# A gated cross-attention and ternary feed-forward block: fewer small instructions, w3 in fp16, one more batch element in Strassen's form

## The chip, the cores and the metric

The kernel runs on one core of a Trainium2 chip. The metric is the device time of one execution in microseconds (us), taken as the median of three runs; the profile is of one more execution. The engines are named as in the profile: PE (TensorE matmuls), PEld (its weight loads), DVE (VectorE), ACT (ScalarE), POOL (GpSimd) and SP (SyncE, whose queue issues every DMA here).

## The reference

The input x is 8 batch elements of 256 x 512, and so is the context. All is float32. Cut to what matters:

```python
# attention, per element; n = layernorm(x), m = context
theta = theta_w @ m + b;  phi = phi_w @ n + b;  g = g_w @ n + b     # latent 128 x 512 each
p     = softmax(theta.T @ phi)                                      # 512 x 512
t     = (p @ g.T).T                                                 # 128 x 512
h     = relu((t - mean(t)) * rsqrt(var(t) + 1e-5) * gamma + beta)
x     = x + tanh(g_xattn) * (out_w @ h + out_b + m)
# feed-forward with ternary weights and 8-bit activations, per row; y = layernorm(x)
bit(y, w) = quant8(rmsnorm(y)) @ ternary(w).T    # ternary: round(w / mean|w|) clipped to -1..1, times mean|w|
x     = x + tanh(g_ffn) * bit(silu(bit(y, w1)) * bit(y, w2), w3)    # w1, w2: 2048 x 512; w3: 512 x 2048
```

## The kernel before

Each batch element b (0 to 7) is held as two tiles of 128 rows by 512 (`x`, `med`). The feed-forward works on 128 rows at a time, numbered i = 2b + c from 0 to 15. All weights are loaded once, scaled, rounded to -1, 0 or 1 and kept on the chip.

The code records about 1500 labelled steps, such as `jtheta0:2` (a projection for element 2), `ug1:7` (the gate matmuls of i = 7, columns 512 to 1023) or `us1:7` (their Silu). A list written out in the source, `order`, says in which sequence the steps are issued, over all engines; each engine runs its own steps in that sequence. A table `alt` puts a step on another engine than its first choice (`v` DVE, `p` POOL, `a` ACT). Tiles come from pools with a fixed number of places by size: `t` (2 KB a partition, 31 places), `f` (4 KB, 7) and `b` (8 KB, 7). A step that takes a place waits until the last reader of what lay there is done, and the instructions behind it on its engine wait with it. That holds for loads in SP's queue too.

The steps that the text speaks of, with their lines in the profile:

- Loads: `x`, `med` (`Lx`, `Lm`), w2T, w1T, w3T in four chunks of 1 MB each (L283, L284).
- Weights: a chunk's sum of absolute values (`ws`, L296 on ACT, L297 on DVE), scaling to int16 (`wr`, L313, L314), sign (`wq`, L320 on ACT, L321 on DVE). w1's and w2's forms are fp16, w3's fp8. For fp8, sums and scaled values go into scratch tiles of 4 KB from pool `f` (`wj`, `wr`); for fp16 they are written where the result goes.
- Attention: layernorm (`nr` L347, `nm` L349, `nx` L352), splits into a high and a low part (`xh`, `xl`, `mh`, `ml`), projections L385, scores L463, maximum L472, exponential L475. For elements 0 and 1 the probabilities are transposed by PE (`pT`, L498), for the others by a DMA (`pt`, L525). Then the mean and variance over the element (L572 to L578, `tr` on L577), output projection L610 with residual L621.
- Feed-forward in: `im` (L651) makes the negated mean, L659 and L661 the statistics, `iz` (L667) the quantized rows, `if` (L680) two scale factors per half, the first of which the Silu reads, `ig` (L682) the reciprocal of the second. A DMA transposes the rows (`it`, L684).
- Up: gate and up matmuls with 512 columns (`fgp`, `fup`, L699), Silu (L709, ACT), product (L711, DVE).
- Quantization of the hidden rows: sum of squares L731, maximum L732, `qf` (L733) and `qe` (L737) from the reciprocal, L734, L735, `qr` L738, power L739, `qb` L740, then scaling `qz` (L745) and a DMA transpose (`qt`, L763).
- Down: 16 matmuls with 512 columns (`fop`, L772, steps `dm`) and a residual (L777). For elements 2 to 6 ("fast") the two halves of an element and the halves of w3 are taken as a 2 x 2 block product in Strassen's form (Winograd's variant): seven products `tP1` to `tP7` of 8 matmuls with 256 columns (`dp`, L857), four sums of the rows (`tS`, L845 on DVE, L846 on POOL), a copy `tC` (L870), four adds from PSUM (`tU`, L864) and two scaled adds (`tA`, L890 on DVE, L892 and L893 on POOL). The sums of w3's blocks (`w3t`; `tW`, L822 on POOL, L823 on DVE) are made once and take one `b` tile for the whole run.

PSUM has eight places of 512 columns, shared by all of PE's results.

```python
_upd(CFG, {..., "bufs": {"t": 31, "f": 7, "b": 7}, "fast": [2, 3, 4, 5, 6], "alt": {...}, "order": [...]})
def tiny(label, fn):
    op(label, v=lambda: fn(V), p=lambda: fn(G))     # a small step, on DVE unless alt says POOL
```

Of the kernel before, what the change touches and what calls it, by code (L numbers as in the profile page):

```python
# [19 lines left out]
P = 128  # L20
# [69 lines left out]
def flamingo_gated_block(  # L90
# [74 lines left out]


    xs = [[w_(f"x{b}_{c}", [P, T]) for c in range(DC)] for b in range(B)]
    meds = [[w_(f"med{b}_{c}", [P, T]) for c in range(DC)] for b in range(B)]
    proj_w = {n: c_(f"{n}_w", [P, DC, L]) for n in ("theta", "phi", "g")}
    proj_src = {"theta": theta_wT, "phi": phi_wT, "g": g_wT}  # L170

    cols, tg = c_("cols", [P, columns.shape[1]]), c_("tg", [P, 2])
    col = {n: (lambda k=k: cols()[:, k : k + 1]) for k, n in enumerate(("theta", "phi", "g"))}
    ob = lambda: cols()[:, 3 : 3 + DC]
    gates = lambda: cols()[:, 3 + DC : 5 + DC]
    gam, bet, ow = c_("gam", [P, T]), c_("bet", [P, T]), c_("ow", [P, D])
    ones, neg_half = c_("ones", [P, P]), c_("neg_half", [P, 2 * DC])

    fac = {n: (c_(f"{n}_max", [P, DC]), c_(f"{n}_sum", [P, 1]), c_(f"{n}_back", [P, 1]), c_(f"{n}_fwd", [P, 1])) for n in ("phi", "g")}
    half_w = {n: c_(f"{n}_half", [P, 2, DC, L], F16) for n in ("phi", "g")}  # L180
    theta_hi, theta_lo = c_("theta_whi", [P, DC, L], F32R), c_("theta_wlo", [P, DC, L], F32R)
    cols2 = c_("cols2", [P, 2])
    bias = {"theta": (lambda: cols2()[:, 0:1]), "phi": (lambda: cols2()[:, 1:2])}

    whole_x = [b for b in range(B) if b not in CFG["xsplit"]]
    whole_m = [b for b in range(B) if b not in CFG["msplit"]]
    assert set(whole_x) <= set(whole_m)
    keep = {"phi": False, "g": any(b not in CFG["p32"] for b in whole_x), "theta": any(b not in whole_x for b in whole_m)}
    scaled_t = {n: c_(f"{n}_sc", [P, DC, L]) if k else w_(f"{n}_sc", [P, 2 * DC, L]) for n, k in keep.items()}
# [19 lines left out]
    def constants():  # L209
        op("C:ones", lambda: V.memset(ones(), 1.0))  # L210
        op("C:half", lambda: V.memset(neg_half(), -0.5))
        if CFG["p32"] or CFG["rpe"]:
            op("C:id0", lambda: G.memset(ident(), 0.0))
            op(
                "C:id1",
                lambda: G.affine_select(
                    out=ident(), in_=ident(), compare_op=ALU.not_equal, fill=1.0, base=0, pattern=[[-1, P]], channel_multiplier=1
                ),
            )
        wps = ps_("warm")  # L220

        op("C:warm", lambda: [PE.matmul(wps()[:, 0:P], ones(), ones(), start=True, stop=True) for _ in range(CFG["warm"])])
        for n in ("theta", "phi", "g"):
            load_proj(n)
        op("Lc:0", lambda: nc.sync.dma_start(out=cols(), in_=columns))
        op("Lgam:0", lambda: nc.sync.dma_start(out=gam(), in_=ln_gamma))
        op("Lbet:0", lambda: nc.sync.dma_start(out=bet(), in_=ln_beta))
        op("Low:0", lambda: nc.sync.dma_start(out=ow(), in_=out_wT))
        op("C:tanh", lambda: S.activation(tg(), gates(), AF.Tanh))
        if CFG["rpe"]:  # L230
            tiny("C:gid", lambda e: e.tensor_scalar(gident(), ident(), tg()[:, 0:1], 1.0, ALU.mult, ALU.mult))

        tiny("C:ow", lambda e: e.tensor_scalar(ow(), ow(), tg()[:, 0:1], 1.0, ALU.mult, ALU.mult))
        op("C:owh", a=lambda: S.copy(ow_hi(), ow()), v=lambda: V.tensor_copy(ow_hi(), ow()))
        tiny("C:owl", lambda e: e.tensor_tensor(ow_lo(), ow(), ow_hi().bitcast(F32), ALU.subtract))
        tiny("C:ob", lambda e: e.tensor_scalar(ob(), ob(), tg()[:, 0:1], 1.0, ALU.mult, ALU.mult))

        for n in ("phi", "g"):
            mx, sm, back, fwd = fac[n]
            tot = ps_(f"{n}_tot")
            op(f"C:{n}max", lambda n=n, mx=mx: V.tensor_reduce(mx(), proj_w[n](), AX.X, ALU.max, apply_absolute_value=True))
            op(f"C:{n}sum", lambda mx=mx, sm=sm: V.tensor_reduce(sm(), mx(), AX.X, ALU.add))
            op(f"C:{n}tot", lambda sm=sm, tot=tot: PE.matmul(tot()[:, 0:1], ones(), sm(), start=True, stop=True))
            lim = 1e-30 if n == "phi" else 1e-2
            op(f"C:{n}back", lambda tot=tot, back=back, lim=lim: V.tensor_scalar(back(), tot()[:, 0:1], lim, 1.0 / G_SCALE, ALU.max, ALU.mult))
            op(f"C:{n}fwd", lambda back=back, fwd=fwd: V.reciprocal(fwd(), back()))
            tiny(f"C:{n}w", lambda e, n=n, fwd=fwd: e.tensor_scalar(scaled_w[n](), proj_w[n](), fwd(), 1.0, ALU.mult, ALU.mult))  # L250
            op(
                f"C:{n}h",
                a=lambda n=n: S.copy(half_w[n]()[:, 0], scaled_w[n]()),
                v=lambda n=n: V.tensor_copy(half_w[n]()[:, 0], scaled_w[n]()),
            )
            tiny(f"C:{n}l", lambda e, n=n: e.tensor_tensor(half_w[n]()[:, 1], scaled_w[n](), half_w[n]()[:, 0], ALU.subtract))
        pback, pfwd = fac["phi"][2:]
        tiny("C:tw", lambda e: e.tensor_scalar(scaled_w["theta"](), proj_w["theta"](), pback(), 1.0, ALU.mult, ALU.mult))
        tiny("C:tb", lambda e: e.tensor_scalar(cols2()[:, 0:1], col["theta"](), pback(), 1.0, ALU.mult, ALU.mult))
        tiny("C:pb", lambda e: e.tensor_scalar(cols2()[:, 1:2], col["phi"](), pfwd(), 1.0, ALU.mult, ALU.mult))  # L260
        op(
            "C:th",
            a=lambda: S.copy(theta_hi(), scaled_w["theta"]()),
            v=lambda: V.tensor_copy(theta_hi(), scaled_w["theta"]()),
        )
        tiny("C:tl", lambda e: e.tensor_tensor(theta_lo(), scaled_w["theta"](), theta_hi().bitcast(F32), ALU.subtract))
        tiny("C:gback2", lambda e: e.tensor_scalar(gback(), fac["g"][2](), 1.0 / P_SCALE, 1.0, ALU.mult, ALU.mult))
# [4 lines left out]
    def weights(n):  # L272
# [30 lines left out]
        if n < 2:  # L303
            op(f"wf:{n}", lambda: V.tensor_scalar(wfac()[:, n : n + 1], wmean()[:, n : n + 1], 1.0 / (127.0 * Q_UNIT), None, ALU.mult))
        else:
            op(f"wf:{n}", lambda: V.tensor_scalar(wmean()[:, 2:3], wmean()[:, 2:3], tg()[:, 1:2], None, ALU.mult))
# [22 lines left out]
    def attention(b):  # L329
        xt, med = xs[b], meds[b]  # L330
        xsp, msp, osp = b in CFG["xsplit"], b in CFG["msplit"], b in CFG["osplit"]
        s32, p32 = b in CFG["s32"], b in CFG["p32"]

        w32 = {
            "phi": proj_w["phi"],
            "theta": scaled_w["theta"] if xsp else proj_w["theta"],
            "g": proj_w["g"] if p32 else scaled_w["g"],
        }
        bias_b = bias if xsp else col

        mv, rstd, nmu = s_("mv", f"mv{b}", [P, DC, 2]), s_("rstd", f"rstd{b}", DC), s_("nmu", f"nmu{b}", DC)
        xn = [w_(f"xn{b}_{c}", [P, T]) for c in range(DC)]
        for c in range(DC):
            st = s_("bst", f"bst{b}_{c}", V.BN_STATS_DIM)
            op(f"nb{c}:{b}", lambda c=c, st=st: V.bn_stats(st(), xt[c]()))  # L345
            op(f"na{c}:{b}", lambda c=c, st=st: V.bn_aggr(mv()[:, c, :], st()))
        tiny(f"nr:{b}", lambda e: e.tensor_scalar(rstd(), mv()[:, :, 1], LN_EPS, 1.0, ALU.add, ALU.mult))  # L347
        op(f"np:{b}", lambda: G.tensor_tensor(rstd(), rstd(), neg_half()[:, :DC], ALU.pow))
        tiny(f"nm:{b}", lambda e: e.tensor_scalar(nmu(), mv()[:, :, 0], -1.0, 1.0, ALU.mult, ALU.mult))  # L349

        def norm(eng, c):
            return eng.tensor_scalar(xn[c](), xt[c](), nmu()[:, c : c + 1], rstd()[:, c : c + 1], ALU.add, ALU.mult)  # L352

# [240 lines left out]
        else:  # L594
# [4 lines left out]
                p=lambda: G.tensor_scalar(h(), h(), 3e38, 0.0, ALU.min, ALU.max),  # L599
            )  # L600

        osums = sums[b] = []
        for c in range(DC):
            o = ps_(f"o_ps{b}_{c}")

# [28 lines left out]
    def ffn_in(b):  # L634
# [10 lines left out]

        for c in range(DC):
            sq = w_(f"fsq{b}_{c}", [P, T])  # L650
            tiny(f"im{c}:{b}", lambda e, c=c: e.tensor_scalar(nmu()[:, c : c + 1], sums[b][c](), -1.0 / T, 1.0, ALU.mult, ALU.mult))  # L651
# [308 lines left out]
```

## Time and profile before

| | before |
|---|---|
| median of three runs (lowest to highest) | 280.13 us (279.75 to 280.41) |
| the profiled execution | 279.37 us |
| its span, first to last instruction | 277.6 us |
| granted clock of PE | 0.999 |
| PE, DVE, ACT, POOL busy | 271.3, 254.0, 227.6, 205.9 us |
| HBM read, written | 22.02 MB, 4.19 MB |

The profile lists what each engine did and when. "Busy" is the union of an engine's instructions; the time that PE's matmuls end is modelled, so its busy share is an upper bound. A group's line gives source line, engine, operation, the tiles and shapes, how often (x), then the busy time in us, the mean duration of one in ns, and the engine's idle time before them. The list of waits gives the engine and line that waited, what ended the wait, the total in us, the number and the longest. The chain of waits is followed back from the last instruction; in order of time each piece has its start and length in us.

### The profile page before, as it was taken

How to read it: one execution, taken by the hardware profiler on the slowest of the kernel's cores; microseconds unless marked ns; L12 is line 12 of the kernel's file. 1: busy time of each engine (PE TensorE's matmuls, PEld its weight loads, DVE VectorE, ACT ScalarE, POOL GpSimd, SP SyncE). 2: the span in 40 equal slices, each digit the busy share in tenths (PEclk: the TensorE clock that was granted, in tenths of full speed). 3: DMA queues.
4: the chain of work that ended last, by engine and by line, in shares of the span. 5: the costliest groups of instructions: out<-in, count | busy, mean ns of one | idle time of the engine just before them, and what ended most of it. 6: DMA issues, size and time to landing. Idle time of an engine off the chain costs nothing.

```text
span 277.6 us, 4741 instructions
## 1 busy us (share of the span) xinstructions
PE 271.3 (98%) x1574; PEld 166.9 (60%) x1574; DVE 254.0 (91%) x537; ACT 227.6 (82%) x337; POOL 205.9 (74%) x273
## 2 busy tenths in 40 slices
PE   7999999999899999999999999999999999999995
PEld 7458585564365555545754778655545566457863
DVE  3798988999999989989999899997999889999895
ACT  1399999999989999899999899895867789675910
POOL 2588774799999998867896989758785855873461
PEclk9999999999999999999999999999999999999999
DMA  7999979998761325134948815916372356605685
GB/s 217 357 347 374 387 277 367 184 195 327 154 115 38 79 41 110 40 76 130 155 97 180 161 41 113 154 34 118 88 142 76 61 130 113 151 2 110 77 211 212
DMA packets 81528, 43.30 MB, mean 156 GB/s; under 512 B 67936, under 2 KB 69088, under 8 KB 81504
## 3 DMA queue, kind: packets, MB, share of 16 engines
q1 hardware_dynamic: 81504, 43.00, 62.2%
q8 instruction: 12, 0.20, 0.3%
q14 instruction: 12, 0.10, 0.1%
HBM read 22.02 MB, written 4.19 MB: 94 GB/s over the span
## 4 chain that ended last, share of the span: by engine, by line
PE 82%; DVE 8%; ACT 3%; issue 2%; DMA 2%; POOL 1%; SPq 0%; POOLq 0%; ACTq 0%
PE fup L699 18%; PE fgp L699 17%; PE dp L857 10%; PE fop L772 6%; PE av L538 4%; PE sc L463 4%; PE phi_ps L385 4%; PE theta_ps L385 3%; PE gx_ps L416 3%; PE tp L498 3%; PE o_ps L610 3%; PE sc L461 3%; PE av L551 3%; DVE nmax L472 2%; DMA med<-in_media 2%
## 5 line engine op out<-in xcount | busy, mean ns | idle before, releaser
L699 PEld LDWEIGHTS <-fqt 128*128 128x128 f16 x512 | 49.0, 99 | 56.8 <-issue 3.2
L699 PE MATMUL fgp<-w1q,fqt 128*128 128x512 f16 x256 | 61.7, 379 | 1.4 <-ACT fh L709 1.4
L699 PE MATMUL fup<-w2q,fqt 128*128 128x512 f16 x256 | 62.3, 379 | 0.0
L709 ACT ACTIVATE fh<-fgp,fback 128x512 f32<-128x512 f32 x64 | 41.1, 687 | 10.4 <-PE fgp L699 8.9
L711 DVE TENSOR_TENSOR fh<-fup,fh 128x512 f32<-128x512 f32 x64 | 42.6, 681 | 2.8 <-PE fup L699 1.6
L732 DVE TENSOR_REDUCE fham<-fh 128x1 f32<-128x2048 f32 x15 | 34.2, 2280 | 0.1
L731 ACT ACTIVATE fhq<-fh 128x2048 bf16<-128x2048 f32 x15 | 28.7, 1913 | 0.4 <-POOL fhfl L733 0.4
L745 ACT ACTIVATE fhq<-fh,fhqs 128x2048 f16<-128x2048 f32 (+1 forms) x14 | 26.6, 1907 | 1.9 <-DVE fhqs L735 1.7
L475 ACT ACTIVATE e<-sc,nmax 128x512 f32<-128x512 f32 x32 | 21.8, 689 | 2.8 <-DVE nmax L472 2.3
L772 PE MATMUL fop<-w3q,fhi 128*128 128x512 fp8e4 (+1 forms) x112 | 22.9, 349 | 0.0
L472 DVE TENSOR_REDUCE nmax<-sc 128x1 f32<-128x512 f32 x32 | 21.6, 681 | 0.7 <-PE sc L463 0.3
L450 POOL TENSOR_TENSOR x<-x,med 128x512 f32<-128x512 f32 x14 | 19.3, 1375 | 3.8 <-ACT med L444 3.7
L519 DVE SCALAR_TENSOR_TENSOR ph<-e,rden,ph 128x512 f16<-128x512 f32 x24 | 17.8, 760 | 0.0
L857 PEld LDWEIGHTS <-fhi 128*128 128x128 f16 x160 | 15.6, 98 | 3.6
L538 PE MATMUL av<-pt,gx 128*128 128x256 f16 x144 | 17.5, 273 | 0.0
L772 PEld LDWEIGHTS <-fhi 128*128 128x128 f16 x112 | 10.6, 98 | 9.3 <-DMA fhi<-fhq 0.4
L538 PEld LDWEIGHTS <-gx 128*128 128x128 f16 x144 | 13.8, 98 | 3.4 <-issue 0.3
L667 POOL TENSOR_SCALAR fq<-x,fnmu,fqs 128x512 f16<-128x512 f32 x16 | 14.1, 889 | 0.8 <-DVE fqs L663 0.2
L654 ACT ACTIVATE fsq<-x,fnmu 128x512 f32<-128x512 f32 x16 | 11.5, 719 | 3.1 <-DVE fnmu L651 2.3
L345 DVE BATCH_NORM_STATS2 bst<-x 128x6 f32<-128x512 f32 x16 | 10.8, 683 | 3.3 <-DMA x<-in_x 3.2
L416 PEld LDWEIGHTS <-xh 128*128 128x128 f16 x144 | 9.4, 98 | 5.5 <-issue 3.3
L621 DVE SCALAR_TENSOR_TENSOR x<-o_ps,x 128x512 f32<-128x512 f32 x16 | 10.9, 687 | 1.9 <-PE o_ps L610 1.6
(223 smaller groups left out, 688.9 us busy)
## 6 DMA issues: line engine op xcount, KB each, us to landing
x<-in_x SPq DMA_DIRECT2D x16, 256.0 KB, 4.0
med<-in_media SPq DMA_DIRECT2D x16, 256.0 KB, 4.5
w<-in_w2T SPq DMA_DIRECT2D x4, 1024.0 KB, 7.7
w<-in_w1T SPq DMA_DIRECT2D x4, 1024.0 KB, 8.2
w<-in_w3T SPq DMA_DIRECT2D x4, 1024.0 KB, 9.7
out<-x SPq DMA_DIRECT2D x15, 256.0 KB, 2.3
fhi<-fhq SPq DMA_TRANSPOSE x17, 4.4
gam<-in_ln_gamma SPq DMA_DIRECT2D x1, 256.0 KB, 10.4
```

The lines of the kernel that those rows point to most:

```text
L385: PE.matmul(ps(), w, v, start=c == 0 and k == 0, stop=c == DC - 1 and k == e)
L472: op(f"sx{t}:{b}", lambda sc=sc, nmax=nmax: V.tensor_reduce(nmax(), sc(), AX.X, ALU.max, negate=True))
L475: lambda t=t, sc=sc, nmax=nmax, e=e: S.activation(e(), sc(), AF.Exp, bias=nmax(), accum_out=den()[:, t : t + 1]),
L538: PE.matmul(av()[:, ts(g, TG * P)], gx()[:, hg, ts(s, L)], v[:, hp, s], start=k == 0, stop=k == 3 * TCH - 1)
L699: PE.matmul(ps(), qt()[:, c * EC + k, :], wq[n][j]()[:, k, :], start=k == 0, stop=k == EC - 1)
L709: lambda j=j, gp=gp: S.activation(h()[:, ts(j, 512)], gp(), AF.Silu, scale=back()[:, c, 0:1]),
L711: op(f"um{j}:{i}", lambda j=j, up=up: V.tensor_tensor(h()[:, ts(j, 512)], up(), h()[:, ts(j, 512)], ALU.mult))
L731: op(f"qs:{i}", lambda: S.activation(hq().bitcast(BF16), h(), AF.Square, accum_out=ss()[:, 0:1]))
L732: op(f"qa:{i}", lambda: V.tensor_reduce(am()[:, 0:1], h(), AX.X, ALU.max, apply_absolute_value=True))
L745: return S.mul(hq()[:, sl], h()[:, sl], qs())
L772: PE.matmul(o()[:, sl], hi()[:, f, :], wq[2][f // 4]()[:, f % 4, sl], start=f == 0, stop=f == FC - 1)
L857: PE.matmul(banks[n]()[:, h * HT : (h + 1) * HT], l()[:, f, :], r(f), start=f == 0, stop=f == HC - 1)
```

## The change

- Small instructions. The negated mean of the layernorm (`nm`) goes: the normalization subtracts the mean itself. `tr` goes: the epsilon is added with the mean (a constant tile `eps2`), and the sign is turned by an operand of the step before. The two `im` of an element become one on 2 columns, the two `if` one on 2 x 2. `qf` goes, its constant being folded into w2's factor, and `qe` is computed once per element (`ge`) in place of once per i.
- w3's ternary form and its block sums are fp16 (`"w16": [0, 1, 2]`), the block sums in two `b` tiles in place of one; w3's sums and scaled values need no scratch tiles.
- Element 1 joins the elements in Strassen's form.
- Pool `t` has 29 places in place of 31, `f` 6 in place of 7, `b` still 7.
- `order` and `alt` are new throughout.

```diff
-"bufs": {"t": 31, "f": 7, "b": 7}, "fast": [2, 3, 4, 5, 6], "alt": ..., "order": ...
+"bufs": {"t": 29, "f": 6, "b": 7}, "fast": [1, 2, 3, 4, 5, 6], "w16": [0, 1, 2], "alt": ..., "order": ...
...
-            op(f"wf:{n}", lambda: V.tensor_scalar(wfac()[:, n : n + 1], wmean()[:, n : n + 1], 1.0 / (127.0 * Q_UNIT), None, ALU.mult))
+            unit = 1.0 / (127.0 * Q_UNIT) / (Q_EPS * RMS_EPS**0.5 if n else 1.0)
+            op(f"wf:{n}", lambda: V.tensor_scalar(wfac()[:, n : n + 1], wmean()[:, n : n + 1], unit, None, ALU.mult))
...
-        tiny(f"nm:{b}", lambda e: e.tensor_scalar(nmu(), mv()[:, :, 0], -1.0, 1.0, ALU.mult, ALU.mult))
-            return eng.tensor_scalar(xn[c](), xt[c](), nmu()[:, c : c + 1], rstd()[:, c : c + 1], ALU.add, ALU.mult)
+            return eng.tensor_scalar(xn[c](), xt[c](), mv()[:, c, 0:1], rstd()[:, c : c + 1], ALU.subtract, ALU.mult)
...
-        op(f"tu:{b}", lambda: V.tensor_scalar(mu(), mps()[:, 0:2], 1.0 / P, None, ALU.mult))
+        op(f"tu:{b}", lambda: V.scalar_tensor_tensor(mu(), mps()[:, 0:2], 1.0 / P, eps2(), ALU.mult, ALU.add))
-        tiny(f"tr:{b}", lambda e: e.tensor_scalar(rs(), var(), -1.0, LN_EPS, ALU.mult, ALU.add))
...
+        tiny(f"im:{b}", lambda e: e.tensor_scalar(nmu(), sums[b](), -1.0 / T, 1.0, ALU.mult, ALU.mult))
-            tiny(f"im{c}:{b}", lambda e, c=c: e.tensor_scalar(nmu()[:, c : c + 1], sums[b][c](), -1.0 / T, 1.0, ALU.mult, ALU.mult))
...
-        for k in range(2):
-            tiny(f"if{k}:{b}", lambda e, k=k: e.tensor_scalar(back()[:, :, k], am(), wfac()[:, k : k + 1], 1.0, ALU.mult, ALU.mult))
+        tiny(f"if:{b}", lambda e: e.tensor_tensor(back()[:, :, 0:2], am().unsqueeze(2).to_broadcast([P, DC, 2]),
+                                                  wfac().unsqueeze(1).to_broadcast([P, DC, 2]), ALU.mult))
+        op(f"ge:{b}", lambda: V.scalar_tensor_tensor(
+            back()[:, :, 3], back()[:, :, 2], 1.0 / Q_EPS**2, back()[:, :, 2], ALU.mult, ALU.mult))
...
-        tiny(f"qf:{i}", lambda e_: e_.tensor_scalar(fl(), back()[:, c, 2:3], Q_EPS * RMS_EPS**0.5, 1.0, ALU.mult, ALU.mult))
-        tiny(f"qe:{i}", lambda e_: e_.tensor_scalar(e(), back()[:, c, 2:3], back()[:, c, 2:3], RMS_EPS, ALU.mult, ALU.mult))
-        tiny(f"qr:{i}", lambda e_: e_.tensor_scalar(r(), ss()[:, 0:1], 1.0 / FF, e(), ALU.mult, ALU.add))
+        tiny(f"qr:{i}", lambda e_: e_.tensor_scalar(r(), ss()[:, 0:1], 1.0 / FF, back()[:, c, 3:4], ALU.mult, ALU.add))
...
-    tw = w_("w3t", [P, 4, HC, HT], F8)
+    tws = [w_(f"w3t{k}", [P, 2, HC, HT], F16) for k in range(2)] if w16 else [w_("w3t", [P, 4, HC, HT], F8)]
```

In the queue of SP, media of element 2 is row 17 (first half) and 21 before, and row 25 and 23 after; the first half then stands behind `x4_0` (the first half of x of element 4, row 24), and both wait for matmuls of L498.

## The prediction

> **What bounds the kernel now.** I read the page's first part and its chain by engine, then the list of PE's waits, then the chain in order of time.
>
> ```profile
> PE 271.3 (98%) x1574; PEld 166.9 (60%) x1574; DVE 254.0 (91%) x537; ACT 227.6 (82%) x337; POOL 205.9 (74%) x273
> PE 82%; DVE 8%; ACT 3%; issue 2%; DMA 2%; POOL 1%; SPq 0%; POOLq 0%; ACTq 0%
> ```
>
> ```profile
> PE fgp L699 <- ACT fh L709: 1.4, 1, 1.4
> PE warm L222 <- DVE neg_half L211: 1.0, 1, 1.0
> PE theta_ps L385 <- DMA med<-in_media: 0.6, 1, 0.6
> ```
>
> TensorE (PE) is busy in 98% of the span, and in all of the run it waits only three times for over half a microsecond: 3.0 us in all, of which 1.6 us lies in the first 7 us. DVE is at 91%, but only 8% of the chain is on it. So what PE has to stream is the floor, and DVE, ACT and POOL matter only where they make PE wait. The chain shows where that is, and at which rate PE streams:
>
> ```profile
> 68.22 1.89 ACT wj L296 x2
> 71.14 1.86 ACT fh L709 x3
> 73.03 1.90 PE fgp L699 x8
> ...
> 116.65 2.59 PE fup L699 x12
> 119.24 2.59 PE fop L772 x12
> ...
> 266.39 1.75 PE dp L857 x16
> 268.14 6.26 PE fop L772 x40
> 274.39 0.03 issue
> 274.42 0.48 DVE x L777
> ```
>
> At 73.03 PE stands still until ACT has done three Silus (L709), queued behind a block sum of w3 (`wj`, L296). From then to 274.39 the chain is PE almost throughout. At the end the last down matmul is followed by one half-width DVE add and the output's DMA: 277.6 - 274.4 = 3.2 us. Twelve fp16 matmuls with 512 columns (`fup`) take 2.59 us, 216 ns each, and twelve fp8 ones (`fop`) the same; sixteen with 256 columns (`dp`) take 1.75 us, 109 ns each.
>
> The profiled execution took 279.37 us (span 277.6, and 1.8 around it); the median of the runs is 280.13, 0.76 above it. I sum changes against 279.37 and move the result up by 0.76. What a measurement of this kernel can tell from no change is about 0.2%, 0.56 us.
>
> **Strassen for element 1.** Out go 2 x 16 down matmuls with 512 columns (i = 2 and 3): 32 x 216 ns = 6.91 us. In come 7 products of 8 matmuls with 256 columns: 56 x 109 = 6.10 us. PE gains 0.81 us, certain as far as PE sets the time. What is added for it lies elsewhere: four sums (L845: 0.7 to 0.8 us on DVE, L846: 2.1 on POOL; the list puts two on each), four bank adds (three of 0.69 and one of 0.42, L864), one copy (0.37), two scaled adds (0.75 on DVE; 0.69 + 1.27 on POOL) in place of two residuals (2 x 0.74): about +3.2 us on DVE and +6.2 on POOL.
>
> **w3 in fp16.** The down matmuls stream fp16 in place of fp8. `fup` against `fop` says 216 against 216 ns: nothing for PE. On the other engines:
>
> ```profile
> L823 DVE TENSOR_TENSOR w3t<-w3q,w3q 128x1024 fp8e4<-128x1024 fp8e4 x2 | 2.4, 1218 | 0.0
> L845 DVE TENSOR_TENSOR sy<-sy,fhi 128x1024 f16<-128x1024 f16 x4 | 3.2, 794 | 0.0
> L320 ACT ACTIVATE w3q<-wr 128x2048 fp8e4<-128x2048 int16 x4 | 7.6, 1901 | 0.0
> L321 DVE TENSOR_SCALAR w2q<-w2q 128x2048 f16<-128x2048 int16 x3 | 2.0, 682 | 0.0
> L737 POOL TENSOR_SCALAR fhe<-fback 128x1 f32<-128x1 f32 x11 | 5.2, 472 | 1.0
> ```
>
> Three of the sign steps go from ACT (1901 ns) to DVE (682): -5.7 us on ACT, +2.0 on DVE. Of the eight subtractions that make `w3t`, DVE had three (2 x 1218, 1426) and gets six at an fp16 price of 0.7 to 0.8: 3.9 becomes 4.6. POOL had five (2.0 to 2.1 each) and keeps two: -6.2. The fp8 intermediates and the 4 KB scratch tiles of w3's sums and products are gone.
>
> POOL's own subtractions took 2012 to 2344 ns (L822), so whatever ran beside them cost 0.33 us at most; at that, six more on DVE slow POOL by 2.0 us, and it stays 2 us below its old load.
>
> The Trainium skill, "GPSIMD Engine Reference", section Specifications, speaks against this move: POOL shares its SBUF interfaces with VectorE, and two-input work on DVE is named among what contends. Held for their whole length, the six would cost POOL an estimated 6 x 0.8 = 4.8 us, and it would end 0.7 us above its old load.
>
> **Small instructions.** 64 go and 10 come, 8 of them per-element squares (`ge`) on DVE, for which the nearest row is L661's 212 ns. On DVE 25 go: L349 5 x 162 ns, L577 2 x 138, L651 7 x 147, L680 2 x 319, L733 4 x 138, L737 5 x 199: 4.3 us, less 1.7 for `ge`. On POOL 39 go, `fhe` (11 x 472) the largest: some 14 us. None stands in a PE wait but through DVE's and ACT's queues. So I put them at nothing on the path; the cover is PE's own streaming, and should that cover be gone, their worth is up to DVE's 2.6 us.
>
> **The order of everything.** The list is new throughout and moves other work too: POOL gains `rx`, `xl`, `ml` and `tA` steps, three `iz` go to DVE. With the row's mean for each instruction of the order lists of both kernels (less the 0.07 us by which neighbours on DVE and ACT overlap, which is their sum less the busy time), DVE changes by -1.0 us, ACT by -4.7, POOL by -4.1.
>
> What decides is whether PE's inputs still come in time. I took each PE instruction that waits for ACT, and from PE's streaming up to it took off ACT's own work up to the instruction that releases it. The least of these leads, before and after: 5.9 and 7.0 us (PE work 40 to 80), 5.8 and 6.7 (80 to 120), 5.2 and 7.1 (120 to 160), 5.1 and 8.8 (160 to 200). For DVE: 7.8 and 9.8, 8.2 and 10.2, 10.8 and 11.7, 11.7 and 12.0, 14.1 and 13.2, 13.2 and 13.5 to the end. So ACT is some 1 us further ahead of PE where the 1.4 us wait stands and 2 to 4 us later on. The factor that opens the first Silu (`if`) stands 1.2 us earlier in DVE's queue. The 73 us wait should shrink: between 0 and -1.5 us, and I take -0.9, a little over half, near the 1.1 that ACT's lead has grown.
>
> **What waits newly.** The pools shrink: `t` 31 to 29, `f` 7 to 6, and `w3t` holds two of the seven `b` tiles in place of one. SP issues in order, so a load that waits for a tile holds all loads behind it. Before, media of element 2 is loaded as row 17 of SP's list without such a wait. Now its first half stands as row 25, behind `x4_0`, and both wait for transposing matmuls (L498) of element 0. PE needs it 3.7 us of its own work later (jtheta0:2, near 30 us). The rows:
>
> ```profile
> x<-in_x SPq DMA_DIRECT2D x16, 256.0 KB, 4.0
> med<-in_media SPq DMA_DIRECT2D x16, 256.0 KB, 4.5
> ```
>
> A median landing of 4.5 us and 0.4 of issue make a wait of 1.2 us; the first x landed in time for a start 2.7 us after its issue (0.72 to 3.38), which makes none. Four w2 chunks are issued earlier now, so the queue is emptier at that point; between 0 and +1.2 I take +0.2. Two transposes are tight as well: `pt2:6` has 5.3 us between the matmul that frees its place and its use, against a landing of 4.4; that fits.
>
> **Sum.** -0.81 - 0.9 + 0.2 = -1.5 us: 279.37 becomes 277.87, and beside the median 278.6 us. With the whole wait at 73 us gone, no new one, and half a microsecond of the small waits on the way (0.2 near 163, 0.2 near 268) it is -2.8 and 277.3.
>
> **Rivals.**
> *Slower: the loads behind the smaller pools.* The media load waits in SP; behind it stand w1's chunks. If the landing takes 6 us as in the full queue (w1's 1 MB takes 8.2), PE stands 2.7 us near 30 us, and ACT, which sums these chunks, passes on the rest at 60 to 75 us, where its lead is only 1 us larger than where it already failed. With the old wait kept, -0.8 + 2.7 + 1 = +2.9: 283.0; with half of the new waits, -0.8 + 1.85 = +1.05: 281.2. It decides once the new waits exceed PE's 0.8 us, the 0.56 that can be told, and what the old wait gives back. For it: every weight load in the first 40 us runs at a DMA share near 1. Against it: ACT's and DVE's leads.
> *No change: PE's 0.8 us is eaten.* The wait at 73 us stays, since ACT's and DVE's queues up to there hold nearly the same work, and 0.3 to 1.2 us of new waits come: 279.6 to 280.7.
> *PE gains nothing.* fp16 could stream slower than fp8 where the weights beside it are fp16; `fop` and `fup` use the same kind of stationary tile and differ by nothing, so I give it no more than a place within the case of no change.
>
> **Chances.** Forecast and its neighbours, 277.0 to 279.5: 0.62. No change: 0.13. Slower: 0.25, of which I put a good half under 282. The likeliest case alone spans 277.2 to 279.5; to hold 8 in 10 the range goes from 277.0 to 282.0. Faster by over 0.2% (under 279.57) 0.62, within it 0.13, slower (over 280.69) 0.25.
>
> **What would show it.** In the page after: PE's busy time about 0.8 us less beside its waits, `dp` at 336 in place of 280, `fop` with 512 columns at 48 in place of 80, all of them fp16, and 216 and 109 ns a matmul in the chain. In PE's waits: the ACT wait near 73 us under 0.8 us, and a DMA wait of theta_ps near 30 us under 0.5. Wrong would be a theta_ps wait of over 1.4 us, an ACT wait on fgp as long as before, or any PE wait behind a transpose between 140 and 180 us. If DVE's or ACT's share of the chain grows beyond 11%, the floor is no longer PE's.

## The result and the profile after

The changed kernel takes 288.60 us (median of 4 runs, 288.44 to 289.57), the kernel before 279.94 beside it (278.88 to 280.41): a ratio of 1.032, 95% interval 1.028 to 1.036. The forecast was 278.6 us and faster; the range up to 282.0 doesn't hold the result.

The profiled execution of the changed kernel took 289.57 us, the longest of the four, with a span of 287.7. Its busy times and its chain by engine:

```profile
PE 273.9 (95%) x1598; PEld 169.5 (59%) x1598; DVE 255.7 (89%) x524; ACT 224.4 (78%) x334; POOL 214.1 (74%) x246
PE 68%; DVE 13%; POOL 5%; DMA 5%; ACT 4%; issue 2%; SPq 1%; ACTq 0%
```

TensorE (PE) has fallen from 82 to 68% of the chain, and GpSimd (POOL), which had 1%, has 5%. POOL has 27 instructions fewer than before (246 against 273) and is busy 8.2 us longer (214.1 against 205.9); the forecast had it 4.1 us shorter. One group explains that. It was L352 in the kernel before (the first line here) and is L355 in the changed kernel (the second):

```profile
L352 POOL TENSOR_SCALAR xn<-x,nmu,rstd 128x512 f32<-128x512 f32 x12 | 10.2, 849 | 1.4 <-PE theta_ps L385 1.0 <-POOL rstd L348 0.2
```

```profile
L355 POOL TENSOR_SCALAR xn<-x,mv,rstd 128x512 f32<-128x512 f32 x13 | 28.5, 2190 | 0.3
```

Same tiles, same shape, same engine: 849 ns became 2190. The edit took out the small instruction that negates the mean, and the normalization subtracts the mean in place of adding its negative. On DVE the same two forms take 540 and 547 ns (medians of 4 and 3). PE's waits of half a microsecond and more in the changed kernel, the longest first:

```profile
PE phi_ps L388 <- POOL xn L355: 2.5, 2, 1.6
PE fup L712 <- DVE w2q L325: 1.6, 2, 1.3
PE mu_ps L574 <- DVE mv L572: 1.5, 2, 1.1
PE fgp L712 <- ACT fh L722: 1.3, 1, 1.3
PE warm L224 <- DVE neg_half L211: 1.0, 1, 1.0
PE sc L466 <- DVE x L623: 0.8, 1, 0.8
PE theta_ps L388 <- DMA med<-in_media: 0.7, 2, 0.4
PE av L541 <- DMA pt<-ph: 0.5, 1, 0.5
```

Before there were three of over half a microsecond, 3.0 us together. The list names POOL's `xn` in its first line only; the others are queues that come late behind it, or that the new order made late by itself. Which is which, the list can't say. The experiments can.

### The profile page after: what moved, and what is told of

The parts are those of the page before. It is cut to its first block, busy times and chain, and to the rows that moved or that the text cites. A ratio compares the mean times of both kernels' runs of the same rounds, so it can differ in the third digit from the quotient of the medians.

```text
span 287.7 us, 4753 instructions
## 1 busy us (share of the span) xinstructions
PE 273.9 (95%) x1598; PEld 169.5 (59%) x1598; DVE 255.7 (89%) x524; ACT 224.4 (78%) x334; POOL 214.1 (74%) x246
## 4 chain that ended last, share of the span: by engine, by line
PE 68%; DVE 13%; POOL 5%; DMA 5%; ACT 4%; issue 2%; SPq 1%; ACTq 0%
PE fup L712 14%; PE fgp L712 14%; PE dp L870 12%; PE theta_ps L388 4%; PE gx_ps L419 4%; PE fop L783 4%; PE sc L466 4%; POOL xn L355 3%; DMA med<-in_media 3%; PE phi_ps L388 2%; PE av L541 2%; PE av L554 2%; PE o_ps L614 2%; DMA x<-in_x 2%; DVE fh L724 2%
## 5 line engine op out<-in xcount | busy, mean ns | idle before, releaser
L712 PE MATMUL fgp<-w1q,fqt 128*128 128x512 f16 x256 | 62.8, 379 | 1.3 <-ACT fh L722 1.3
L722 ACT ACTIVATE fh<-fgp,fback 128x512 f32<-128x512 f32 x64 | 41.7, 693 | 6.7 <-PE fgp L712 6.6
L756 ACT ACTIVATE fhq<-fh,fhqs 128x2048 f16<-128x2048 f32 (+1 forms) x15 | 28.8, 1919 | 4.2 <-DVE fhqs L747 4.1
L355 POOL TENSOR_SCALAR xn<-x,mv,rstd 128x512 f32<-128x512 f32 x13 | 28.5, 2190 | 0.3
L870 PEld LDWEIGHTS <-fhi 128*128 128x128 f16 x192 | 18.5, 98 | 4.2 <-issue 0.7
L453 POOL TENSOR_TENSOR x<-x,med 128x512 f32<-128x512 f32 x15 | 20.4, 1368 | 0.2
L783 PE MATMUL fop<-w3q,fhi 128*128 128x512 f16 (+1 forms) x80 | 15.3, 337 | 0.0
L664 POOL TENSOR_TENSOR fr<-fz,neg_half 128x4 f32<-128x4 f32 x8 | 9.4, 1177 | 7.5 <-DVE fz L663 5.5
L750 POOL TENSOR_TENSOR fhr<-fhr,neg_half 128x1 f32<-128x1 f32 x16 | 10.2, 636 | 5.1 <-DVE fhr L749 4.9
L363 POOL TENSOR_TENSOR xh<-xn,xh 128x512 f16<-128x512 f32 x11 | 13.0, 1188 | 0.2
```

Of the source, the lines that this page charges most:

```text
L355: return eng.tensor_scalar(xn[c](), xt[c](), mv()[:, c, 0:1], rstd()[:, c : c + 1], ALU.subtract, ALU.mult)
L712: PE.matmul(ps(), qt()[:, c * EC + k, :], wq[n][j]()[:, k, :], start=k == 0, stop=k == EC - 1)
L722: lambda j=j, gp=gp: S.activation(h()[:, ts(j, 512)], gp(), AF.Silu, scale=back()[:, c, 0:1]),
L756: return S.mul(hq()[:, sl], h()[:, sl], qs())
L783: PE.matmul(o()[:, sl], hi()[:, f, :], wq[2][f // 4]()[:, f % 4, sl], start=f == 0, stop=f == FC - 1)
L870: PE.matmul(banks[n]()[:, h * HT : (h + 1) * HT], l()[:, f, :], r(f), start=f == 0, stop=f == HC - 1)
```

## The experiments

Fourteen kernels ran. Ratios are against the kernel before, run beside each on the same chip; its median lay between 279.52 and 279.76 us beside the experiments. The four-form kernel below ran once and has no ratio.

| kernel | median, us | ratio (95%) |
|---|---|---|
| changed kernel | 288.60 | 1.032 (1.028 to 1.036) |
| changed, add form back (e1_add_back) | 281.12 | 1.0042 (1.0028 to 1.0057) |
| before, subtract form alone (e3_sub_alone) | 286.06 | 1.0225 (1.0199 to 1.0250) |
| changed, subtract in elements 0 to 2 only (e7_sub_early) | 284.97 | 1.0177 (1.0153 to 1.0201) |
| changed, subtract in elements 3 to 7 only (e8_sub_late) | 285.38 | 1.0189 (1.0161 to 1.0216) |
| before, 40 small instructions fewer (e4_small_out) | 281.57 | 1.0058 (1.0036 to 1.0080) |
| the same without `ge` (e10_small_no_ge) | 280.55 | 1.0034 (1.0020 to 1.0049) |
| e1_add_back, old small instructions back (e5_small_back) | 284.35 | 1.0163 (1.0143 to 1.0183) |
| e1_add_back, no Strassen in element 1 (e11_no_strassen1) | 282.12 | 1.0087 (1.0071 to 1.0103) |
| e1_add_back, one sign step on ACT (e6_sign_on_act) | 279.89 | 1.0012 (1.0002 to 1.0022) |
| the same, three places earlier (e9_sign_earlier) | 279.41 | 0.9990 (0.9978 to 1.0002) |
| e9_sign_earlier, two more moves (e12_best) | 281.73 | 1.0066 (1.0044 to 1.0089) |
| e9_sign_earlier, `if:0` early (e13_if_alone) | 280.38 | 1.0028 (1.0014 to 1.0042) |
| e9_sign_earlier, `if:0` less early (e14_if_later) | 279.45 | 0.9994 (0.9984 to 1.0004) |

**The form of the normalization.** The changed kernel with the add form back, the order list untouched:

```diff
-        tiny(f"nr:{b}", lambda e: e.tensor_scalar(rstd(), mv()[:, :, 1], LN_EPS, 1.0, ALU.add, ALU.mult))
+        tiny(f"nr:{b}", lambda e: [
+            e.tensor_scalar(rstd(), mv()[:, :, 1], LN_EPS, 1.0, ALU.add, ALU.mult),
+            e.tensor_scalar(nmu(), mv()[:, :, 0], -1.0, 1.0, ALU.mult, ALU.mult)])
...
-            return eng.tensor_scalar(xn[c](), xt[c](), mv()[:, c, 0:1], rstd()[:, c : c + 1], ALU.subtract, ALU.mult)
+            return eng.tensor_scalar(xn[c](), xt[c](), nmu()[:, c : c + 1], rstd()[:, c : c + 1], ALU.add, ALU.mult)
```

> The changed kernel, but with the normalization in its old form: the step that makes 1/sigma's argument issues a second small instruction that writes the negated mean to a tile of its own, and the normalization adds it in place of subtracting the mean out of `mv`. The order list is untouched. Theory (GpSimd's normalization in the subtracting form costs 2.1 us in place of 0.8, and that is what the forecast missed): `xn` on GpSimd falls back to 0.76-0.85 us, GpSimd's busy time falls by 14 to 17 us, and the time is 278 to 281 us, 7.5 to 10.5 below the changed kernel. Rival 1 (the new order, the smaller pools or the sixth Strassen element cost the time, and the long normalizations lie beside other work): `xn` gets short all the same, but the time stays at 286 to 289 us. Rival 2 (`xn` is long because of what runs beside it in the new order, not because of its form): `xn` stays near 2 us and the time at 288.

281.12 us, just over the 281 given: 2.8% of the time is back. The group and all of PE's waits of over 0.3 us in this run:

```profile
L362 POOL TENSOR_SCALAR xn<-x,nmu,rstd 128x512 f32<-128x512 f32 x13 | 11.6, 895 | 0.3
```

```profile
PE fup L719 <- DVE w2q L325: 1.6, 2, 1.3
PE fgp L719 <- ACT fh L729: 1.3, 1, 1.3
PE warm L224 <- DVE neg_half L211: 1.0, 1, 1.0
PE av L548 <- DMA pt<-ph: 0.4, 1, 0.4
```

Eight small instructions are back and POOL is busy 199.1 us, 15.0 less. The waits behind `xn`, `mv` and `x` are gone, so all three were the long normalization's, and those for media are too short to be listed. Both rivals fall. The waits for `w2q`, the Silu and `pt` stay: those belong to the rest of the change.

The next run asks what makes it long: the subtraction, or the mean read out of `mv`, where the columns of a chunk stand two apart.

```diff
+        form = ("ss", "sc", "as", "ac")[b % 4]
...
-            return eng.tensor_scalar(xn[c](), xt[c](), mv()[:, c, 0:1], rstd()[:, c : c + 1], ALU.subtract, ALU.mult)
+            mean = mv()[:, c, 0:1] if form[1] == "s" else nmu()[:, c : c + 1]
+            return eng.tensor_scalar(xn[c](), xt[c](), mean, rstd()[:, c : c + 1], ALU.add if form[0] == "a" else ALU.subtract, ALU.mult)
```

> The changed kernel with the normalization in four forms, by element: 0 and 4 as changed (mean out of `mv`, whose columns stand two apart, subtract); 1 and 5 subtract, but the mean copied first to a tile of its own; 2 and 6 add, the negated mean written back into `mv`; 3 and 7 add, the negated mean in a tile of its own (the old form). Theory A (GpSimd's subtract is slow): 0, 4, 1, 5 near 2.1 us, 2, 6, 3, 7 near 0.77 us. Theory B (GpSimd is slow with the scalar read out of `mv`): 0, 4, 2, 6 near 2.1 us, 1, 5, 3, 7 near 0.77 us. If it's neither but what runs beside them, no pattern by element. I hold A at 0.7. The time is not what this run is for: between 280 and 286 us.

From the timeline of POOL in that run (start and length in us), in order: elements 1 (subtract, own tile), 2 (add, out of `mv`), 4 (subtract, out of `mv`) and 7 (add, own tile):

```profile
12.99 4.14 POOL L372 TENSOR_SCALAR xn<-x,nmu,rstd 128x512 f32<-128x512 f32 x2
...
18.77 0.77 POOL L372 TENSOR_SCALAR xn<-x,mv,rstd 128x512 f32<-128x512 f32 x1
...
74.19 2.08 POOL L372 TENSOR_SCALAR xn<-x,mv,rstd 128x512 f32<-128x512 f32 x1
...
153.48 1.97 POOL L372 TENSOR_SCALAR xn<-x,nmu,rstd 128x512 f32<-128x512 f32 x2
```

All six that subtract took 2.07 to 2.51 us, all seven that add 0.76 to 1.22, wherever the mean lay. It is the subtraction (theory A). This single run took 284.95 us.

The one part alone, in the kernel before: `nm` issues nothing, and the normalization is that of the changed kernel.

```diff
-        tiny(f"nm:{b}", lambda e: e.tensor_scalar(nmu(), mv()[:, :, 0], -1.0, 1.0, ALU.mult, ALU.mult))
+        op(f"nm:{b}", lambda: [])
```

> The kernel before, with this one part of the change alone: the eight small instructions that negate the mean are left out and the normalization subtracts the mean out of `mv`. Order list, pools, formats and Strassen elements are those of before. Theory: the 12 normalizations on GpSimd go from 0.77-0.85 to about 2.1 us, 15 to 17 us more of GpSimd, of which the first ones (13 us into the run, with little work for TensorE yet) come straight onto the path at 1.3 us each; 283 to 289 us, 3 to 9 above before. Rival (only in the new order do they matter): within 1 us of before.

286.06 us, 2.25% above before, as the theory had it:

```profile
L352 POOL TENSOR_SCALAR xn<-x,mv,rstd 128x512 f32<-128x512 f32 x12 | 25.6, 2137 | 1.0 <-PE theta_ps L385 0.7
```

Where in the run does it cost? Two runs of the changed kernel subtract in some elements only (`form = "ss" if b < 3 else "ac"`, and the other way round):

> The changed kernel with the subtracting normalization only in elements 0 to 2 (5 on GpSimd, at 6 to 29 us); elements 3 to 7 add the negated mean. Theory: these five come while TensorE has little else to do, and each comes onto the path: 5 x 1.3 = 6.5 us less what waits beside them; of the 7.5 us between the changed kernel and e1_add_back, 3.5 to 6 come back: 284.5 to 287. Rival (the later ones cost as much, by holding GpSimd's and DVE's queues): 282 to 284.

> The other half: the subtracting normalization only in elements 3 to 7 (8 on GpSimd, at 70 to 160 us); elements 0 to 2 add. Theory: here TensorE has other elements' work, and the eight cost 1.5 to 4 us together: 282.5 to 285. If the two halves are separate costs, their excesses over 281.1 add up to the 7.5 us of all; if they come to much less or more, the two halves share a wait or make one another longer.

284.97 and 285.38 us, 3.85 and 4.26 above e1_add_back: together 8.1, against 7.5 for all. So the two halves are nearly separate costs. The later eight cost a little more than the 4 us given (285.38 against 285), though each of them less than one of the early five (0.5 against 0.8 us). The early five put 2.1 us into PE's waits behind `xn`, and in that execution PE also waits 1.2 us for media at 34 us, which it doesn't in e1_add_back; in e8_sub_late there is neither, and its own lines are

```profile
PE mu_ps L591 <- DVE mv L589: 1.3, 2, 0.9
PE sc L483 <- DVE x L640: 0.8, 1, 0.8
```

These are DVE's steps behind late work of POOL. The chain back from the longer `mv` wait, at 144.5 us, runs over POOL's normalizations at 130.5 and 136.9; ahead of `x`, two DVE steps (L853, L875) take 1.52 and 1.67 us, against 0.75 and 0.69 in e1_add_back. The profiled execution is the fastest of its four (283.88 us), so the list may leave out part of the cost.

**The small instructions.** The kernel before without `tr`, `qf`, `qe` and one of the two `if`, with `ge`; each step that is out issues nothing, so the order stays:

```diff
-        tiny(f"qe:{i}", lambda e_: e_.tensor_scalar(e(), back()[:, c, 2:3], back()[:, c, 2:3], RMS_EPS, ALU.mult, ALU.mult))
+        op(f"qe:{i}", lambda: [])
...
+        # behind ig, in the same step
+                V.scalar_tensor_tensor(back()[:, :, 3], back()[:, :, 2], 1.0 / Q_EPS**2, back()[:, :, 2], ALU.mult, ALU.mult),
```

> The kernel before without most of the other small instructions that the change takes out: the 8 `tr`, 16 `qf`, 16 `qe` and 8 of the 16 `if` are gone, the 8 squares `ge` come in behind the reciprocals, the two memsets of `eps2` too; the negated means and the two `im` per element stay, and so do order, pools and formats. Theory (on record: they lie beside TensorE's streaming): 40 instructions less, DVE and GpSimd together some 10 us shorter, the time within 0.8 us of before. Rival (they lengthen DVE's and GpSimd's queues on the path): 1 to 3 us faster. A second rival (one of the new forms is as dear on GpSimd as the normalization's): 1 us slower or more, and the row of `fback` or `rs` on GpSimd shows it.

It got slower by 0.6%, which neither the theory nor the first rival had (the second had the size, but not the rows: `fback` on POOL takes 0.2 to 0.7 us), though POOL is busy 11.0 us less (194.9). PE's wait of 1.4 us at 73 us is gone; in its place are four of about 0.5 us, at 69, 73, 165 and 216 us. `ge` takes 452 ns on average here, where the forecast had 212. One of them on DVE, and what POOL does at that time:

```profile
203.26 1.11 DVE L695 SCALAR_TENSOR_TENSOR fback<-fback 128x2 f32<-128x2 f32 x1
```

```profile
203.08 1.27 POOL L908 TENSOR_TENSOR x<-sy,x 128x512 f32<-128x512 f32 x1
```

POOL's addition ends at 204.35, and the square of two columns, 0.16 us at its shortest, ends at 204.37: it stood still until POOL was done.

The same without `ge` (`qe` stays):

> e4_small_out without its new squares: `qe` stays as it was (16 small instructions), `ge` doesn't come in; `tr`, `qf` and half of `if` are out as there. Theory (what e4_small_out lost is `ge`, which DVE ran in 0.45 us on average, two of them in 1.1 to 1.2 us, each ending within 0.02 us of the end of a long two-input instruction of GpSimd): 279.2 to 280.2, back at the time of before. Rival (the loss is in the new meeting points of DVE and GpSimd in an order made for other instructions, whichever instruction it is that meets): it stays 1 to 2 us above before, 280.7 to 281.7.

280.55 us lies between the two expectations: `ge` may be worth some 0.24% (1.0058 against 1.0034, but the intervals overlap), the rest stays. Nothing singles out what the rest is; PE's waits in that run, beside the one at its start, are five of 0.2 to 0.5 us, behind ACT, DVE and DMAs.

And the old small instructions back in the new order, each ahead of the instruction that needs it:

> The run with the added negated mean (e1_add_back, 281.12 us), and all the other old small instructions back as well, each on the engine and at the place of the instruction that needs it: `tr` ahead of `tp`, two in place of one for `if`, `qf` ahead of `qm`, `qe` ahead of `qr`, no `ge`. The order list is that of the changed kernel. Theory (the small instructions lie beside TensorE's streaming; what e4_small_out lost comes from where an order made for other instructions falls): within 0.8 us of 281.1. Rival (the new small instructions cost by themselves, above all `ge` on DVE, which took 0.44 us on average with single ones of 1.2 and 2.0 us, where the forecast had 0.21): 1 to 2 us faster, about 279.5.

284.35 us: 3.2 slower than e1_add_back, against both expectations (the theory within 0.8, the rival 1 to 2 faster). New among PE's waits are

```profile
PE theta_ps L395 <- POOL dg L498: 1.2, 1, 1.2
PE fgp L715 <- DVE fh L727: 0.9, 1, 0.9
```

So small instructions are not free in either order: taking 40 out of an order made with them cost 1.6 us (0.58%), putting them into an order made without them 3.2. Whether their lengths or their new places do it, these two runs don't part.

**Strassen for element 1.** e1_add_back with two plain down projections for element 1, at the places of the products (`"fast": [2, 3, 4, 5, 6]`):

> e1_add_back with element 1 back to two plain down projections: the 32 matmuls with 512 columns stand where the seven products stood, the two residuals where sums of the products were, and the four sums, four bank adds, the copy and the two scaled adds are left out. All else is as in e1_add_back (281.12 us). Theory (on record: TensorE gains 6.91 - 6.10 = 0.81 us by Strassen's form, and the sums lie beside its streaming): 281.5 to 282.3. Rival (the 3.2 us on DVE and 6.2 us on GpSimd that come with it cost as much as it gains): 280.4 to 281.2.

282.12 us, 0.45% (1.0087 against 1.0042) or 1.3 us above e1_add_back. The product form does gain; the two intervals leave 0.4 to 2.1 us for it, so it can't be told from the 0.81 us of PE's streaming.

**The order around the first Silu.** In e1_add_back PE waits 1.6 us for `w2q`. The stretch of DVE's timeline ahead of it:

```profile
55.85 1.09 DVE L658 TENSOR_SCALAR fnmu<-osum 128x2 f32<-128x2 f32 x1
56.85 1.28 DVE L482 TENSOR_REDUCE nmax<-sc 128x1 f32<-128x512 f32 x2
58.05 1.36 DVE L325 TENSOR_SCALAR w1q<-w1q 128x2048 f16<-128x2048 int16 x1
...
60.52 1.27 DVE L325 TENSOR_SCALAR w2q<-w2q 128x2048 f16<-128x2048 int16 x1
...
62.44 2.36 DVE L325 TENSOR_SCALAR w2q<-w2q 128x2048 f16<-128x2048 int16 x2
```

A sign step takes 0.68 us where nothing holds it; here they take 1.36, 1.27 and, for the last two together, 2.36. `fnmu`, 0.15 us a column in the kernel before, takes 1.09. That is 3.3 us over the price in 10 us, all beside POOL's work. The first run on this moves one sign step of w2 (`wq1:1`) from DVE back to ACT:

```diff
-"wq1:1": "v"
+"wq1:1": "a"
```

> e1_add_back with one step on another engine: the sign step of w2's second block (`wq1:1`), which the change moved from ACT to DVE and at which TensorE waits 1.5 us at 61.9 us, back on ACT, at the same place of the order. Theory (the list gives DVE more than it can do between 41 and 65 us, and the forecast's leads missed that since they took DVE's own work at the row's mean, without the time that it's held while GpSimd works): TensorE's wait for `w2q` (1.6 us listed, 1.9 with the second) falls below 0.8, the wait for the first Silu (1.3) shrinks too, and the time is 1 to 2 us lower, 279.1 to 280.1. Rival (the wait is only moved, since ACT gets 1.9 us more in the stretch ahead of the first Silu): within 0.5 us of 281.1, with a longer wait behind ACT.

279.89 us, 1.2 less, as the theory had it. Then the same step ahead of two squares on ACT:

> e6_sign_on_act with the same sign step three places earlier in ACT's list, ahead of the two squares of element 1 (`iq0:1`, `iq1:1`) in place of behind them. In e6_sign_on_act ACT stands idle for 0.86 us there, waiting for `fnmu`, while this step's input has lain ready since about 45 us; behind it TensorE waits 0.5, 0.7 and 0.6 us for `w2q`, `tx` and the first Silu (2.3 us by its starts). Theory (these three waits hang on ACT's queue between 57 and 68 us): all of ACT from there on is 0.9 us earlier, the three waits shrink to 0.3 to 1 us together, and the time is 278.2 to 279.2, 0.7 to 1.7 below e6_sign_on_act and 0.2 to 0.5% faster than the kernel before. Rival (DVE then sets the same waits): within 0.4 us of 279.9.

279.41 us. The wait for `w2q` is gone, those for `tx` and the Silu are 0.4 and 1.0. It is 0.5 us less than e6_sign_on_act, between the two expectations. ACT is earlier, but ahead of the first Silu's table load it now stands idle for 0.70 us, waiting for DVE. The interval holds 1, so it can't be told from the kernel before.

Two further moves, `tx:2` ahead of `wr2:0` on ACT and `if:0` (which opens the first Silu) early on DVE, made it worse:

> e9_sign_earlier with two more steps moved in the order list. On ACT `tx:2` goes ahead of `wr2:0`: it frees a PSUM bank for which TensorE waits 0.5 us at 62.9 us, its own input is there at 59.9 us, and the rounding of w1 (2.0 us), behind which it stands, is needed only at 65.5 us. On DVE `if:0`, which opens the first Silu, goes from behind eight other steps to right behind `ib:0`, where its inputs lie ready: 61.5 us in place of 64.9. Theory (these two hang on the order alone): the wait at 62.9 us goes, and the first Silu's table load starts when ACT is free, 0.7 us earlier, so that its wait falls from 1.15 to 0.3 to 0.6 us; 278.0 to 278.9, 0.2 to 0.5% faster than before. Rival (what comes next on DVE or GpSimd sets the same time): 279.2 to 279.6, the time of e9_sign_earlier.

281.73 us, above both expectations. PE waits 2.4 us in one piece for a PSUM bank that DVE's `gx` (L438) gives back, and then streams at half rate. The windows of PE in this run (length and busy us, matmuls, granted clock, DMA share, GB/s):

```profile
66.00:68.00 2.00, 0.67 (x4) 1.00 1.05 392
68.00:70.00 2.00, 2.00 (x7) 0.53 0.74 265
70.00:72.00 2.00, 2.00 (x9) 0.62 0.00 0
72.00:74.00 2.00, 2.00 (x11) 1.00 0.39 78
```

One of the moves alone:

> e9_sign_earlier with one of the two moves of e12_best: `if:0` on DVE right behind `ib:0`; `tx:2` stays where it was on ACT. In e12_best TensorE waited 2.4 us in one piece for a PSUM bank (`gx`, L438) and then streamed eight matmuls at 427 ns in place of 216. Theory A (that wait comes from moving `tx:2`, which changes the order in which PSUM banks are given back): here it doesn't appear, the first Silu's table load starts when ACT is free, 0.7 us earlier than in e9_sign_earlier, and the time is 278.4 to 279.2. Theory B (it comes from `if:0`, or the first Silu is set by ACT's and DVE's work together whichever step goes first): 279.2 to 279.8, with TensorE's wait behind ACT as long as before (1.15 us by its starts).

280.38 us, above both expectations. The PSUM wait doesn't appear, so it takes the move of `tx:2`; whether that alone makes it wasn't run. The Silu's table load starts 0.74 us earlier, as theory A had it (64.78 against 65.52), but a new wait of 0.7 for `w2q` takes its place. The sign steps of both runs on DVE and what POOL does, e9_sign_earlier first:

```profile
61.54 1.29 DVE L325 TENSOR_SCALAR w2q<-w2q 128x2048 f16<-128x2048 int16 x2
```

```profile
61.52 1.79 POOL L455 TENSOR_SCALAR med<-med,tg,cols 128x512 f32<-128x512 f32 x1
```

```profile
62.16 2.36 DVE L325 TENSOR_SCALAR w2q<-w2q 128x2048 f16<-128x2048 int16 x2
```

```profile
62.31 1.65 POOL L460 TENSOR_TENSOR x<-x,med 128x512 f32<-128x512 f32 x1
```

In the first DVE goes through in 2 x 0.68 us (less the overlap) and POOL's step, 0.77 us elsewhere in that run, takes 1.79. In the second, 0.6 us later, POOL's `x<-x,med` (1.27 us elsewhere) begins during the first sign step, and the second sign step goes on only after its end: it ends 0.56 us behind it. The last run puts `if:0` behind the sign steps:

> e9_sign_earlier with `if:0` on DVE behind the two sign steps of w2 in place of ahead of them (e13_if_alone): it lies where DVE waits for `tx` anyway, and the sign steps start at 61.5 us as in e9_sign_earlier, ahead of GpSimd's `x<-x,med`. Theory (what e13_if_alone lost is that the sign steps, 0.6 us later, met `x<-x,med` on GpSimd: one took 1.75 us in place of 0.68): here both take 0.68 us, the first Silu's table load starts 0.7 us earlier than in e9_sign_earlier, and the time is 278.4 to 279.2, under both kernels. Rival (any move here makes some other pair of DVE and GpSimd steps meet): 279.4 to 280.4, with another DVE row lengthened to GpSimd's end.

279.45 us. The sign steps are at 0.69 and 0.68 again, and the Silu's wait is 0.3 in place of 1.0, as the theory had it; the time is not: 0.9994 (0.9984 to 1.0004), in the rival's range. The profiled execution of this kernel, the slowest of its 13 (280.86 us), has a wait that e9_sign_earlier's hasn't:

```profile
PE theta_ps L395 <- DMA med<-in_media: 1.4, 1, 1.4
```

It stands at 32 us, ahead of everything that differs between the two kernels: the media of element 2 took 5.0 us to land here and 3.6 there. So it comes and goes between executions, and the trace doesn't say where the 0.7 us went. No version was found that is faster than the kernel before by more than its measurement can tell.

## Why the prediction was wrong

**The step that failed** is the order list's sum: "With the row's mean for each instruction of the order lists of both kernels". It priced the changed `xn` by the row of the old one, 849 ns, and took the eight `nm` out as a gain "at nothing on the path". The edit had changed the operation, and no row of the trace showed a POOL normalization that subtracts. Such a price has to be bounded from both sides. The rows of L360, POOL's subtractions with two inputs of that size, gave 1.16 to 1.29 us; even that end, 13 x 0.3 to 0.4 = 4 to 6 us more of POOL, would have been a rival's mechanism. The real price, 2190, makes 13 x 1.34 = 17.4 us. Of the 10.0 us between forecast and result, 7.5 are this (e1_add_back), and it works in the old order as well (6.3 us, e3_sub_alone).

**The leads** are the second step. The forecast took off "ACT's own work", and DVE's, each at the row's mean, and had DVE's least lead to 80 us grow from 7.8 to 9.8. PE then waited 1.6 us for DVE's `w2q`. The leads left out the time in which DVE stands still while POOL works; e6_sign_on_act shows that this queue was overfull. That this is all they left out isn't shown: the runs show 3.3 us of it in 10 us, against a least lead put at 9.8. **The wait at 73 us** was to shrink by 0.9; it stayed (1.3 against 1.4), which the prediction named as a sign of being wrong. A `pt` wait of 0.4 to 0.6 came between 134 and 143 us, at 142.9 in the changed kernel, inside the stretch where it was another such sign. Without the subtraction the kernel is 1.4 us above before (281.12 against 279.76) in place of 1.5 below. These three terms, 1.6 + 0.9 + 0.4, have the size of that difference of 2.9, but that they are it is argued: only the first was tested (1.2 us, e6_sign_on_act), and other waits changed too, such as before's 0.6 for media at 6.5 us.

**The small instructions** "at nothing": their sum on DVE was bounded by 2.6 us, which e5_small_back (3.2) exceeds, and e4_small_out turns the sign round (taking them out cost 1.6). So their own length doesn't give the price; that it lies in which instruction they meet or push fits the squares that POOL held, and is not shown for the rest.

**Right** were the terms on PE. Sixteen fp16 products take what the fp8 ones took, and Strassen's gain is there (e11_no_strassen1). From the chain of the changed kernel:

```profile
273.79 1.75 PE dp L870 x16
```

The new load wait near 30 us, put between 0 and 1.2 with +0.2 taken, is 0.2 in the profiled execution of the changed kernel, nothing in those of e1_add_back and e9_sign_earlier, and 1.2, 1.0 and 1.4 in those of e7_sub_early, e12_best and e14_if_later; what it costs in a median isn't shown. Of the rivals, "slower" had its mechanism there, the loads behind the smaller pools, but not the cost, 0.2 of the 10.0 us in the changed kernel; the range's upper end of 282.0 was built on it. In "no change", the upper end of 280.7 doesn't come out of its terms, which give 280.13 - 0.81 + 1.2 = 280.5; nothing hangs on that. The sign that the prediction named last, DVE's share of the chain over 11%, did come (13%).

**A page of the Trainium skill weighed there.** The prediction cited "GPSIMD Engine Reference", Specifications, against moving w3's subtractions to DVE, and took 0.33 us as the most that POOL's neighbour costs. The runs show more. The square of e4_small_out (above) is held for nearly 1 us and ends 0.02 us after POOL's instruction; in e1_add_back, at 250.67 us, another takes 2.01. "SBUF — State Buffer", Who interferes with whom, states such a rule: a DVE instruction in a two-port mode, or with two SBUF inputs against a GpSimd one that reads SBUF, and the GpSimd one exclude each other for the whole instruction, and the one that starts first goes through. The two pairs of lines of e9_sign_earlier and e13_if_alone agree that either engine can hold the other; in the first, POOL's record begins 0.02 us before DVE's and DVE goes through, so the records don't settle which started first. "For the whole instruction" the runs don't bear out beside POOL's subtracting normalization (last section).

## What to carry to other kernels

An edit that takes an instruction out by changing the form of another has to be priced for the new form on every engine that runs it; where the trace has no row of that form on that engine, the price is open, however alike the two look. Here 8 instructions of 0.16 to 0.19 us were saved for 13 that grew by 1.3 us.

Where DVE and POOL work side by side, a sum of row means is not a queue's length: an order fits only with its own meeting points, so a step that is taken out or moved by half a microsecond can cost more than it weighs. What a part of such a change did in the old order (the subtraction 6.3 us) was not what it did in the new one (7.5).

## What was not expected of the hardware

- POOL's `tensor_scalar` on 128x512 f32 takes 0.77 us with add and then multiply and 2.08 us with subtract and then multiply; DVE's takes 0.54 in both. Why, no run shows: POOL's subtraction of two such tiles (L360) takes 1.16 to 1.29 us, about as long as its addition (1.27).
- Many small DVE instructions of two columns, 0.15 us by themselves, took 0.3 to 2.0 us when they began during one of POOL's wide elementwise instructions, and ended with it. Not all: reciprocals of two columns took 0.15 us beside the same kind (in the changed kernel at 189.35 us, beside 2.12 us of POOL).
- Beside the subtracting normalization it depends on the place. In the changed kernel, in one of 2.10 us, a square that began 0.24 us into it took 0.55 us and ended 1.30 before its end, and one that began 1.31 us into it took 0.15; in another of 2.08 us a two-column step that began 1.47 us into it took 0.63 and ended 0.02 us after it. So this form doesn't hold DVE for its whole length.
- PE's granted clock can fall to half after a wait. In the profiled execution of the changed kernel, after waits of 1.6 and 0.9 us close together:

```profile
16.00:18.00 2.00, 1.07 (x3) 0.94 1.05 386
18.00:20.00 2.00, 2.00 (x9) 0.50 1.05 388
20.00:22.00 2.00, 2.00 (x5) 0.71 1.06 388
22.00:24.00 2.00, 2.00 (x11) 1.00 1.04 383
```

That is some 3.4 us at half rate, 1.7 us of streaming lost; e12_best shows the same 3.4 us after its wait of 2.4. In e7_sub_early two waits of 1.2 and 0.9 us at the same place left the clock at 1.00, and so did single ones of 1.3 to 1.5 us in e1_add_back and e3_sub_alone. The other three runs of the changed kernel, with a granted clock of 0.998 to 1.0 over the span, are 0.9 to 1.1 us shorter than the profiled one (0.994); such a loss would do for that, but it isn't shown to be the cause.
